# Moving the state copies of a selective scan from VectorE to ScalarE, and the written order that goes with it

## The chip, the cores and the metric

The kernel runs on one core of a Trainium2 chip. A time is the device time of one execution in microseconds. Lower is better. Of the kernel before there are three runs without the profiler and one profiled execution.

## What is computed

Four layers follow one another on an image of 4 x 64 x 64 positions with 128 channels. Layers 0 and 1 each hold a selective scan over the 4096 positions in four directions (row by row, column by column, and both backwards); layer 2 is a graph-like layer with gates over 3 x 3 neighbours, layer 3 is neighbourhood attention over 7 x 7 windows. The change concerns the scans alone. Cut to what matters:

```python
delta = jax.nn.softplus(dts)                 # per channel and position
A = -jnp.exp(A_logs)                         # per channel and state, 16 states
def step(h, inp):
    d, u, b, c = inp
    dA = jnp.exp(d[..., None] * A)
    h = dA * h + (d * u)[..., None] * b[:, :, None, :]
    y = jnp.sum(h * c[:, :, None, :], axis=-1)
    return (h, y)
```

Layer 0 scans 128 channels, layer 1 scans 256. Around the scans there are projections, a depthwise 3 x 3 convolution, normalizations and gates.

## The kernel before, in words

**Units.** A task is one batch and one block of 128 channels: 4 tasks for layer 0, 8 for layer 1. A task has 16 steps, four directions by four stretches of 1024 positions. A step has 16 units; a unit is 8 channels by 16 states, so 128 partitions, by 1024 positions. That makes 3072 units, and `Scans.run` (L477) is one loop over them, u. `manual_schedule` keeps every engine's instructions in the order in which they are written.

**A unit's work.** `load` (L388) brings the unit's delta times x from DRAM, repeated over the states (dub). `times_b` (L395) multiplies it by B on POOL into dbu, of which there are 3 buffers. `decay` (L400) spreads delta over the states by two matmuls into da, a PSUM tile of two banks with 2 buffers, and ScalarE takes the exponential in place, with A as its scale. `scan` (L410) then does three things on VectorE: the scan itself (L418), in place in da; a copy of the last column (the first, when the direction runs backwards) into states (L428), which the same unit of the next step takes as its initial value; and the product with C (L430) into hc, of which there are 6 buffers. The copy is left out in the last step of each direction, so three steps in four have it. da comes free for unit u+2 when the readers of unit u are done.

**Sums.** `add_up` (L448) sums over states on TensorE into yps, four units at a time and one half of the 1024 positions after the other. `sum_so_far` (L432) puts the y of earlier directions into yps at the start of a step, and `keep` (L463) copies yps to y on ScalarE at its end.

**Order.** In iteration u the loop writes scan(u), keep(u-2), times_b(u+3), decay(u+2), the sums, then the slot for other work, then load(u+6).

**Other work.** Into the slot go the pieces of `prepare` (L286; delta, its three bf16 parts and the repeats of B and C for a later step) and of the side work (`Side`: projections, normalizations, depthwise convolutions, what stands before and after the scans). Both are generators. Each yields the engine that its next piece needs (TAB means an activation from another table, with a table load on either side). `Plan` (L115) keeps a model clock, `at`, for PE, ACT and POOL; `slot` (L153) sets it anew in every unit from now = u x UNIT and adds the unit's own work. `Lane.fits` (L172) lets a piece in when its start plus its usual time is no later than now + UNIT + SLACK of its engine. `Counted` (L75) passes the instructions on and adds their modelled time; this is why all of other work has line L98. DMA issues of other work are put into SP's queue by `post` and `flush` when they are due by the same clock. Pieces of prepare are also forced through by their count, and side work by its pace and due times.

Of the kernel before, what the change touches and what calls it, by code (L numbers as in the profile page):

```python
# [26 lines left out]
NG = 16  # L27
TS = 1024
HALVES = TS // T
# [74 lines left out]
    return int(np.prod(t.shape[1:]))  # L104


UNIT = 3.85
USUAL = dict(PE=2.1, ACT=0.7, TAB=3.3, POOL=1.3)
SLACK = dict(PE=1.2, ACT=2.2, POOL=3.0)
LANDING = 6.0  # L110
FOUR_LANDING = 12.0
ROWS_LANDING = 12.0
# [2 lines left out]
class Plan:  # L115
# [20 lines left out]
    def post(self, chain, issue, due=0.0):  # L136

        if self.running:
            self.posted.append((chain, max(self.done, due), issue))
        else:  # L140
            issue()
# [11 lines left out]
    def slot(self, u, sums):  # L153
        at = self.at
        self.now = u * UNIT
        self.flush()
        at["PE"] = max(at["PE"], self.now) + 1.1
        at["ACT"] = max(at["ACT"], at["PE"]) + 1.1
        at["POOL"] = max(at["POOL"], self.now - 1.2) + 2.4
        at["PE"] += sums  # L160


class Lane:
# [8 lines left out]
    def fits(self, more=0.0):  # L172

        plan = self.plan
        for what in self.next.split():
# [3 lines left out]
            start = max(plan.at[kind], self.ready)  # L179
            if start + USUAL[what] > plan.now + UNIT + SLACK[kind] + more:  # L180
                return False
# [58 lines left out]
class Scans:  # L240
# [45 lines left out]
    def prepare(self, t, step):  # L286
# [40 lines left out]
        def repeat(i):  # L327
            rep = out["BC"[i]] = self.tile("rep" + "BC"[i], 2)
            src = bass.AP(xdd.tensor, xdd.offset + (R + i * NS) * TS, [[TS, NS], [0, 8], [1, TS]])
            nc.sync.dma_start(out=rep, in_=src)  # L330

        for i, free in enumerate((5, 8)):
            post("rep", lambda i=i: repeat(i), max(begin + free * UNIT, ready))

# [34 lines left out]
        def own(part, j):  # L369
            if j == part == 0:  # L370
                out["delta"] = self.tile("dp", 2, shape=(96, 4, TS), dtype=BF16)
            nc.sync.dma_start(
                out=out["delta"][32 * part : 32 * part + 32, j, :], in_=parts[32 * j : 32 * j + 32, part, :]
            )

        for i in range(12):
            j, part = divmod(i, 3)
            post("rep", lambda part=part, j=j: own(part, j), begin + (9 + 0.7 * i) * UNIT)
        yield ""
# [30 lines left out]
    def scan(self, u):  # L410
        nc = self.nc
        t, step, jj, j, g = self.unit(u)
        back = t.steps[step][0] >= 2
        way = slice(None, None, -1) if back else slice(None)
        if g == 0:
            t.states[step] = self.tile("state", 2, shape=(P, NG))
        da, dbu = self.live.pop(("da", u)), self.live.pop(("dbu", u))
        nc.vector.tensor_tensor_scan(  # L418
            da[:, way],
            da[:, way],  # L420
            dbu[:, way],
            0.0 if step % NSTEP == 0 else t.states[step - 1][:, g : g + 1],
            ALU.mult,
            ALU.add,
        )
        if step % NSTEP < NSTEP - 1:
            end = 0 if back else TS - 1
            nc.vector.tensor_copy(t.states[step][:, g : g + 1], da[:, end : end + 1])  # L428
        hc = self.live["hc", u] = self.tile("hc", 6)
        nc.vector.tensor_mul(hc, da, t.prepared[step]["C"])  # L430

# [45 lines left out]
    def run(self, between):  # L477

        total = NU * len(self.tasks)
        first = self.tasks[0]  # L480
        for _ in self.fetch(first):
            pass
        for _ in self.prepare(first, 0):
            pass
        self.plan.start()
        pieces, fetch = Lane(self.plan, iter(())), iter(())
        for u in range(-6, total):
            if u >= 0:
                self.scan(u)
            if u >= 2:  # L490
                self.keep(u - 2)
            if 0 <= u + 3 < total:
                self.times_b(u + 3)
            if 0 <= u + 2 < total:
                self.decay(u + 2)
            if u >= 0 and u % NG in (2, 3):
                self.sum_so_far(u, u % NG - 2)
            if u >= 0 and u % 4 == 3:
                self.add_up(u, 0)
            if u > 0 and u % 4 == 0:  # L500
                self.add_up(u - 1, 1)
            self.plan.slot(u, (1.6 if u % 4 in (0, 3) else 0.0) + (2.1 if u % NG in (2, 3) else 0.0))
            ahead, rest = divmod(u + AHEAD, NG)
            if rest == 0:
                while pieces.step():
                    pass
                self.plan.flush("prep", "rep")
            if rest == 0 and 0 < ahead < total // NG:
                n, step = divmod(ahead, NU // NG)
                if step == 0:  # L510
                    self.plan.flush("side")
                    fetch = self.fetch(self.tasks[n])
                    for _ in range(self.tasks[n].W.nct):
                        next(fetch, None)
                pieces = Lane(self.plan, self.prepare(self.tasks[n], step))
            next(fetch, None)
            while (pieces.count < rest - 2 or pieces.fits()) and pieces.step():
                pass
            if u >= 0:
                n, i = divmod(u, NU)  # L520
                if self.later:
                    self.later.pop(0)()
                between(n, i)
            if 0 <= u + 6 < total:
                self.load(u + 6)
        self.add_up(total - 1, 1)
        self.keep(total - 1)
        while self.later:
            self.later.pop(0)()
# [891 lines left out]
def layer2(tc, C, nb, x_in, x_out, d_w, d_rel, d_v):  # L1421
    with ExitStack() as es:
# [11 lines left out]

        with tc.manual_schedule():
            run(each(E.statistics, 0, range(8)))
            E.roots([E.rstd])
            run(each(E.project, 0, range(6)))
            E.edge_row()
            run(each(E.statistics, 1, range(2)))  # L1440
            before = last = None
            for b in range(nb):
# [392 lines left out]
```

## Time and profile before

| What | Value |
|---|---|
| median of 3 runs | 14696.81 us (14688.04 to 14710.08) |
| the profiled execution's own time | 14702.13 us |
| its span | 14700.3 us |
| mean granted TensorE clock | 0.711 |
| busy: PE, DVE, ACT, POOL | 10730.8, 12416.1, 7877.7, 9851.6 us |
| first and last start of L418 | 310.9 and 11716.3 us (the wait ahead of the first included) |
| L428, state copies | 2304, median 158 ns |
| L408, exponentials | 3072, mean 1089 ns |
| L398, times_b | 3072, mean 2354 ns |
| POOL L398 waiting for DVE L418 | 882.7 us |
| POOL L398 waiting for DMA of dub | 559.2 us |
| ACT casts to parts waiting for POOL | 278.3 us |

A row of the profile's groups gives line, engine, operation, tiles written and read, shapes and count, then busy time and mean duration, then the engine's idle time just before these instructions and what ended most of it. In a timeline, a row begins with start and duration in microseconds from the span's start, and an idle time of the engine ahead of it stands in brackets, with what ended it. Equal neighbours are merged. Waits of an engine for its own queue are not shown.

Up to 11720 us the page shows the scans, with preparation and side work between their units; after that come layers 2 and 3.

### The profile page before, as it was taken

Reading aid. Unit: us, or ns where it says so; the run is one execution under the profiler, and the core shown is the slowest. Engines: PE = TensorE matmul, PEld = TensorE weight load, DVE = VectorE, ACT = ScalarE, POOL = GpSimd, SP = SyncE. Lnnn points to the kernel's source line nnn. Section 1 sums busy time; section 2 is a strip of 40 time slices with the busy share of each in tenths; the row PEclk is TensorE's granted clock in tenths of the full one; section 3 lists DMA queues with packets and bytes.
Section 4 is the critical chain, followed back from the end, with each engine's and each line's share of the span. In section 5 each row is a group of like instructions: output and inputs, shape, how many; then the busy total and the mean of one; then the engine's idle time right before and its main releaser. Section 6 shows DMA issues by size and latency. Waiting matters only on the chain. (4 is left out here: it accounts for less than half of the span.)

```text
span 14700.3 us, 125581 instructions
## 1 busy us (share of the span) xinstructions
PE 10730.8 (73%) x36776; PEld 2755.0 (19%) x36776; DVE 12416.1 (84%) x10627; ACT 7877.7 (54%) x9279; POOL 9851.6 (67%) x4742
## 2 busy tenths in 40 slices
PE   5777777777776677777767767777776657777999
PEld 1111111111111111111111111111111112223555
DVE  1999999999999999999999999999999904565666
ACT  3645466555656565566555555555555335543555
POOL 1877788777888788788778888888888713441000
PEclk7676676766667666667667776667766568777999
DMA  4888888888888988988888777787787600002000
GB/s 113 220 207 218 204 216 222 216 214 217 216 224 215 224 208 208 230 217 211 216 213 213 199 195 200 197 208 200 196 205 193 166 30 24 20 18 48 13 14 8
DMA packets 853732, 2490.00 MB, mean 169 GB/s; under 512 B 143031, under 2 KB 164287, under 8 KB 844855
## 3 DMA queue, kind: packets, MB, share of 16 engines
q1 hardware_dynamic: 853047, 2481.97, 67.1%
q8 instruction: 295, 4.83, 0.1%
q14 instruction: 390, 3.19, 0.1%
HBM read 2060.21 MB, written 270.27 MB: 159 GB/s over the span
## 5 line engine op out<-in xcount | busy, mean ns | idle before, releaser
L398 POOL TENSOR_TENSOR dbu<-dub,repB 128x1024 f32<-128x1024 f32 x3072 | 7189.7, 2354 | 1511.2 <-DVE da L418 882.7
L418 DVE TENSOR_TENSOR_SCAN da<-da,state,dbu 128x1024 f32<-128x1024 f32 x2304 | 5415.4, 2350 | 297.3 <-ACT da L408 246.7
L408 ACT ACTIVATE da<-da,av 128x1024 f32<-128x1024 f32 x3072 | 3343.2, 1089 | 3647.8 <-PE da L406 3582.6
L406 PE MATMUL da<-dp,spread 96*128 96x512 bf16 x6144 | 2592.8, 516 | 2982.7 <-DVE hc L430 2959.1
L430 DVE TENSOR_TENSOR hc<-da,repC 128x1024 f32<-128x1024 f32 x3072 | 3741.0, 1218 | 40.5 <-PE ms L98 0.5
L453 PE MATMUL yps<-hc,gather 128*32 128x512 f32 x12288 | 2363.5, 852 | 2.3 <-DVE hc L430 2.3
L418 DVE TENSOR_TENSOR_SCAN da<-da,dbu 128x1024 f32<-128x1024 f32 x768 | 1759.2, 2291 | 400.7 <-POOL dbu L398 321.5
L406 PEld LDWEIGHTS <-spread 96*128 96x128 bf16 x6144 | 477.5, 107 | 6516.1 <-DVE hc L430 4124.8
L98 PE MATMUL ms<-d,wts 128*128 128x512 f32 (+3 forms) x960 | 782.0, 941 | 203.6 <-POOL d L98 140.7
L98 ACT ACT_TABLE_LOAD x640 | 821.1, 1283 | 126.8 <-DMA xcd<-o 90.8
L98 POOL TENSOR_TENSOR delta<-delta,low 128x1024 f32<-128x1024 f32 x192 | 452.3, 2356 | 529.9 <-ACT low L98 529.9
L98 PE MATMUL mp<-xd,dtw 8*128 8x512 f32 (+1 forms) x768 | 668.9, 965 | 28.7 <-DMA xd<-xdd 17.1
L98 ACT CAST parts<-delta 128x1024 bf16<-128x1024 f32 x384 | 400.5, 1043 | 295.8 <-POOL delta L98 278.3
L1371 POOL TENSOR_TENSOR acc<-acc,part 128x512 f32<-128x512 f32 x256 | 318.8, 1268 | 338.1 <-DVE part L1367 338.0
L446 PE MATMUL yps<-y,ident 128*128 128x512 f32 x576 | 520.3, 998 | 3.2 <-ACT y L471 3.2
L453 PEld LDWEIGHTS yps<-hc,gather 128*32 128x32 f32 x12288 | 283.9, 128 | 1190.3 <-issue 1184.5
L98 POOL TENSOR_TENSOR low<-delta,xc 128x1024 f32<-128x1024 f32 x192 | 501.1, 2610 | 1.7
L1615 ACT ACTIVATE s<-s,nmax 128x512 f32<-128x512 f32 x512 | 366.8, 718 | 248.7 <-DVE nmax L1612 243.9
L1282 ACT ACTIVATE hid<-hid,relb 128x1024 f32<-128x1024 f32 x288 | 320.3, 1145 | 323.0 <-DVE hid L1277 320.3
L98 ACT ACTIVATE low<-mp,av 128x512 f32<-128x512 f32 x384 | 264.1, 688 | 399.9 <-PE mp L98 397.7
L1277 DVE TENSOR_TENSOR hid<-cen,near 128x1024 f32<-128x1024 f32 x288 | 336.2, 1218 | 163.6 <-PE cen L1270 113.6
L98 PE MATMUL ms<-pad,diag 96*32 96x504 f32 (+1 forms) x2304 | 420.4, 824 | 64.0 <-ACT o L98 47.9
(230 smaller groups left out, 11780.3 us busy)
## 6 DMA issues: line engine op xcount, KB each, us to landing
dub<-dud SPq DMA_DIRECT2D x3072, 512.0 KB
dp<-parts SPq DMA_DIRECT2D x2304, 64.0 KB
repB<-xdd SPq DMA_DIRECT2D x192, 512.0 KB
repC<-xdd SPq DMA_DIRECT2D x192, 512.0 KB
dud<-low SPq DMA_DIRECT2D x192, 512.0 KB
pad<-xid SPq DMA_DIRECT2D x192, 256.0 KB
szd<-o SPq DMA_DIRECT2D x96, 256.0 KB
xcd<-o SPq DMA_DIRECT2D x96, 256.0 KB
```

The source lines that it names most:

```text
L98: return call(*args, **kw)
L398: self.nc.gpsimd.tensor_mul(dbu, self.live.pop(("dub", u)), t.prepared[step]["B"])
L406: self.nc.tensor.matmul(da[:, cols], self.C.spread[:, jj, :], dp[:, j, cols], start=True, stop=True)
L408: self.nc.scalar.activation(da, da, AF.Exp, scale=t.W.a[:, at : at + 1])
L418: nc.vector.tensor_tensor_scan(da[:, way], da[:, way], dbu[:, way], 0.0 if step % NSTEP == 0 else t.states[step - 1][:, g : g + 1], ALU.mu ...
L430: nc.vector.tensor_mul(hc, da, t.prepared[step]["C"])
L446: self.nc.tensor.matmul(out, lhs, self.view(rhs, k, c, i, HALVES), start=True, stop=False)
L453: self.nc.tensor.matmul(self.live["yps"][32 * j : 32 * j + 32, cols], self.C.gather[:, jj, :], self.live["hc", v][:, cols], start=False, s ...
L1277: nc.vector.tensor_add(hid.rearrange("p i (r w) -> p (i r) w", w=HW), cen[pair].rearrange("p i (r w) -> p (i r) w", w=HW), self.near[m][s] ...
L1282: nc.scalar.activation(hid, hid, AF.Gelu, bias=self.relb[:, m, t : t + 1])
L1371: nc.gpsimd.tensor_add(acc, acc, part)
L1615: nc.scalar.activation(s[:, i, :], s[:, i, :], AF.Exp, bias=nmax[:, h : h + 1], accum_out=total[:, h : h + 1],)
```

## The change

The state copy goes from VectorE to ScalarE. In the loop, decay moves from behind scan(u), as decay(u+2), to ahead of scan(u), as decay(u+1); so on ScalarE the order is the exponential of u+1, the state copy of u, keep, then the slot's work. keep, sum_so_far and add_up are written one iteration later, and the flush after the loop has both halves of the last sum. times_b and load stay where they are. In the plan UNIT goes from 3.85 to 3.7, ScalarE's slack from 2.2 to 2.4, and the model clock of ACT has a floor for the copy; POOL's line stays.

```diff
-UNIT = 3.85
+UNIT = 3.7
 USUAL = dict(PE=2.1, ACT=0.7, TAB=3.3, POOL=1.3)
-SLACK = dict(PE=1.2, ACT=2.2, POOL=3.0)
+SLACK = dict(PE=1.2, ACT=2.4, POOL=3.0)
...
         at["PE"] = max(at["PE"], self.now) + 1.1
         at["ACT"] = max(at["ACT"], at["PE"]) + 1.1
+        at["ACT"] = max(at["ACT"], self.now + 2.4) + 0.2
         at["POOL"] = max(at["POOL"], self.now - 1.2) + 2.4
         at["PE"] += sums
...
             end = 0 if back else TS - 1
-            nc.vector.tensor_copy(t.states[step][:, g : g + 1], da[:, end : end + 1])
+            nc.scalar.copy(t.states[step][:, g : g + 1], da[:, end : end + 1])
         hc = self.live["hc", u] = self.tile("hc", 6)
         nc.vector.tensor_mul(hc, da, t.prepared[step]["C"])
...
         for u in range(-6, total):
+            if 0 <= u + 1 < total:
+                self.decay(u + 1)
             if u >= 0:
                 self.scan(u)
-            if u >= 2:
-                self.keep(u - 2)
+            if u >= 3:
+                self.keep(u - 3)
             if 0 <= u + 3 < total:
                 self.times_b(u + 3)
-            if 0 <= u + 2 < total:
-                self.decay(u + 2)
-            if u >= 0 and u % NG in (2, 3):
-                self.sum_so_far(u, u % NG - 2)
-            if u >= 0 and u % 4 == 3:
-                self.add_up(u, 0)
+            if u >= 0 and u % NG in (3, 4):
+                self.sum_so_far(u, u % NG - 3)
             if u > 0 and u % 4 == 0:
-                self.add_up(u - 1, 1)
-            self.plan.slot(u, (1.6 if u % 4 in (0, 3) else 0.0) + (2.1 if u % NG in (2, 3) else 0.0))
+                self.add_up(u - 1, 0)
+            if u > 1 and u % 4 == 1:
+                self.add_up(u - 2, 1)
+            self.plan.slot(u, (1.6 if u % 4 in (0, 1) else 0.0) + (2.1 if u % NG in (3, 4) else 0.0))
...
-        self.add_up(total - 1, 1)
+        for i in range(HALVES):
+            self.add_up(total - 1, i)
         self.keep(total - 1)
```

## The prediction

> **What bounds the kernel now.** I read the page's slices and groups first, then VectorE's timeline in a stretch without stalls, then the list of waits, then two stretches of all engines. From the page:
>
> ```profile
> DVE  1999999999999999999999999999999904565666
> L418 DVE TENSOR_TENSOR_SCAN da<-da,state,dbu 128x1024 f32<-128x1024 f32 x2304 | 5415.4, 2350 | 297.3 <-ACT da L408 246.7
> L430 DVE TENSOR_TENSOR hc<-da,repC 128x1024 f32<-128x1024 f32 x3072 | 3741.0, 1218 | 40.5 <-PE ms L98 0.5
> ```
>
> VectorE is full through four fifths of the span. Those are the 3072 scan units, from 320.0 us to 11719.9 us by the first and last rows of L418 and L430: 3.711 us a unit. The rest (layers 2 and 3) is untouched. So the question is VectorE's period per unit. Its timeline, start and duration first:
>
> ```profile
> 5049.53 2.36 DVE L418 TENSOR_TENSOR_SCAN da<-da,state,dbu 128x1024 f32<-128x1024 f32 x1 [0.58 <-ACT da L408]
> 5051.92 0.16 DVE L428 COPY state<-da 128x1 f32<-128x1 f32 x1
> 5051.99 1.22 DVE L430 TENSOR_TENSOR hc<-da,repC 128x1024 f32<-128x1024 f32 x1
> 5053.13 2.35 DVE L418 TENSOR_TENSOR_SCAN da<-da,state,dbu 128x1024 f32<-128x1024 f32 x1
> 5055.51 1.22 DVE L430 TENSOR_TENSOR hc<-da,repC 128x1024 f32<-128x1024 f32 x1
> 5056.65 2.35 DVE L418 TENSOR_TENSOR_SCAN da<-da,state,dbu 128x1024 f32<-128x1024 f32 x1
> ```
>
> With the state copy a unit takes 3.60 us, without it (every fourth step) 3.52. The copy is busy 0.16 us but overlaps: the product starts 0.110 us after the scan's end with it and 0.035 without (medians over all units). It costs **0.075 us** a unit. Above this pace there are 445 us of VectorE stalls in all, mostly ScalarE's exponential arriving late; the list of waits has that, and one line from layer 3 that matters below:
>
> ```profile
> DVE da L418 <- ACT da L408: 321.6, 314, 8.3
> ACT inv L1641 <- PE ps L1639: 26.6, 52, 3.3
> ```
>
> **What the Trainium skill says.** "PSUM — Partial Sum Buffer", section "PSUM bank collisions raise a hardware error": two engines may not touch one bank and 32-partition quadrant at once, two reads included, and accesses are to be guarded by bank, not address. The trace shows that the program is ordered this way: L1641 reads ps[:, 0, :], yet what releases it is L1639, which writes ps[:, 1, :], other columns of the same bank. No row shows two readers. "ScalarE: Activation LUTs", section "What ACT_TABLE_LOAD costs", gives 186 ns plus 0.833 ns per element for an ACTIVATE with immediates and 1283 ns for a table load; here PSUM copies of 512 and 128 elements take 587 and 267 ns (the same slope, 160 ns at zero elements), and the load takes 1283. The PSUM page's "Engine vs sequencer instructions" calls ScalarE's queue strictly first in, first out; the rows below agree.
>
> **The change, part by part.**
>
> *The copy leaves VectorE.* Gain 2304 x 0.075 = 173 us if nothing takes its place. But da lies in two PSUM banks and the product L430 reads both. The copy on ScalarE, written ahead of it, reads a column of one. So I expect **the product to wait for the copy**: the 0.110 us between scan and product becomes hand-off to ScalarE, copy, hand-off back. VectorE to ScalarE takes 0.035 us (L1277 to L1282) or 0.095 (L1612 to L1615), the copy 0.161 (from the line above), ScalarE to VectorE 0.033 (L1641 to L1643) or 0.103 (L408 to L418). Sum 0.229 to 0.359, net of 0.110: +0.12 to +0.25 us; I take 0.17. **2304 x 0.17 = 390 us** (274 to 574).
>
> *The copy sits behind the next unit's exponential.* Until now an exponential had until its own scan starts. Now exp(u+1) must be over when scan(u) ends, 1.2 us earlier, or it holds the copy, and the copy holds product u. A place where this costs nothing today:
>
> ```profile
> 5098.79 1.28 ACT L98 ACT_TABLE_LOAD   x1
> 5100.02 2.35 DVE L418 TENSOR_TENSOR_SCAN da<-da,state,dbu 128x1024 f32<-128x1024 f32 x1
> 5100.08 0.69 ACT L98 ACTIVATE o<-ms,v 128x512 f32<-128x512 f32 x1
> 5100.79 1.28 ACT L98 ACT_TABLE_LOAD   x1
> 5102.08 1.09 ACT L408 ACTIVATE da<-da,av 128x1024 f32<-128x1024 f32 x1
> 5102.40 1.23 DVE L430 TENSOR_TENSOR hc<-da,repC 128x1024 f32<-128x1024 f32 x1
> ```
>
> A Silu between two table loads (3.26 us) delays the exponential to 5103.17, 0.8 us after the scan's end at 5102.37; VectorE doesn't notice, as the next scan starts at 5103.54. In a copying unit the product would have been held 0.8 us. Taking end of exp(u+1) minus end of scan(u) from these rows for every unit: it is over zero in 45% of all, and in 1062 of the 2304 copying ones; in a quiet unit it is -0.48. The positive part sums to 1026 us over copying units; 311 of this is stall of the next scan that is paid today already, leaving 715. A hold lets ScalarE and TensorE catch up, so lateness that carries from one unit to the next counts once: 489. Two corrections oppose each other: the unit is 0.17 us longer, which takes some 100 us off; and side work now begins after the copy, 0.7 us later than after the exponential. Side work that fits a unit without a hold shrinks from 4.2 us to 2.45 (from the copy's end, 2.5 us after the last product, to 4.9): 67 stretches between exponentials hold more than 4.2 today, 368 in copying steps hold more than 2.4, by 333 us in sum. The planner's new lines do not forbid that: ACT work may end at now + 6.1 (3.7 + 2.4) where the held product asks for 4.9 (now is the last product's end; scan(u+1) ends 6.0 us later, and exp(u+2) ahead of its copy takes 1.09). I take **550 us** (350 to 900).
>
> *Decay moved to the head of the loop.* The da matmul and exponential keep their order among themselves, as sums, written one unit later, keep theirs against the da matmuls. What moves is **side work and preparation**: on PE and ACT they now stand one exponential earlier, while POOL's stand behind the same times_b, which waits for the same scan; the plan's POOL line (now - 1.2) is not moved. So a POOL result used by ACT or PE arrives a unit later in their terms:
>
> ```profile
> 5113.80 2.36 POOL L398 TENSOR_TENSOR dbu<-dub,repB 128x1024 f32<-128x1024 f32 x1 [1.56 <-DVE da L418]
> 5116.13 2.34 POOL L98 TENSOR_TENSOR delta<-delta,low 128x1024 f32<-128x1024 f32 x1
> 5118.51 1.05 ACT L98 CAST parts<-delta 128x1024 bf16<-128x1024 f32 x1 [1.73 <-POOL delta L98]
> 5119.46 1.08 ACT L408 ACTIVATE da<-da,av 128x1024 f32<-128x1024 f32 x1
> 5121.96 2.29 DVE L418 TENSOR_TENSOR_SCAN da<-da,dbu 128x1024 f32<-128x1024 f32 x1
> ```
>
> Standing one exponential earlier, this cast would hold the exponential of the scan at 5118.43 until about 5119.6: 2.3 us late. Over the 587 such hand-offs (380 casts, 72 ACT and 135 PE users of side tiles) the same reckoning gives 747 us if POOL keeps its times; 433 if POOL's backlog (times_b starts 2.7 us after its scan in the median) shrinks as VectorE is held; 156 if POOL also gains what it waits for ACT today. Many fall into holds already counted: **200 us** (50 to 450).
>
> *Other edits, together.* keep moves from ahead of an exponential to behind the copy (stalls in that slot are 109 us now, units 3 of 16): no more than it gives back, as 1.47 us of y copy still stands in the shorter window. SP's stores and dub loads keep their order against POOL; 67 us of scan waits for dbu should fade with longer units: -50 us. The smaller UNIT packs side work no more loosely: nothing. The matmul of da(u+2) also waits for the copy now, which is over before product u: nothing.
>
> Sum: 14702.1 (span 14700.3 plus 1.8 around it) + 390 + 550 + 200 - 50 = 15792, less 5 for the median of the runs: **15,790 us**.
>
> **Rivals.**
> 1. *Hand-off only.* The planner's new ACT floor keeps exponentials early enough: 14697 + 390, and up to half of the 550: 15,090 to 15,350. For it: in 55% of units the exponential is early. Against: 300-odd table-load pairs of 3.26 us exceed 2.45.
> 2. *The product does not wait* (faster). Two reads are left unordered; the copy is hidden: 14697 - 173, and 60 off for the keep slots: about 14,460; with some POOL lateness, 14,600. It decides if the product starts about 0.035 us after the scan. For it: no row shows two readers ordered. Against: the skill's rule and L1641.
> 3. *No wait, but POOL lateness rules:* 14697 - 173 + 200 to 430 = 14,720 to 14,950.
> 4. *Everything adds:* no catching up, 574 + 900 + 450: 16,600.
>
> **How the numbers follow.** Forecast 0.65 (own range 15,350 to 16,400), rival 1 0.17, rival 2 0.05, rival 3 0.05, rival 4 0.08. The range 15,150 to 16,450 leaves out rivals 2 and 3, most of 4 and an edge of 1. A difference of 0.2% (30 us) is about what can be told from none. Faster is rival 2, 0.05; the same 0.02, an edge of 3; slower 0.93.
>
> **What would show it.** Right: L430 shows idle time released by an ACT row of the copy line, some 900 us or more; the product starts 0.25 us or more after the scan in copying steps and 0.035 in others; units in copying steps are longer than 3.59 us even without stalls of the scan; ACT casts and PE side matmuls wait longer for POOL. Wrong: L430 without such waits (rivals 2 and 3), or waits of 0.2 us with no long tail (rival 1).

## The result, and the profile after

The change is slower: 15,767.88 us in the median of 4 runs (15,763.88 to 15,777.51), 14,697.60 us before; the ratio is 1.0729, interval 1.071 to 1.0747. The prediction was 15,790 us. The profiled execution took 15,764.78 us, of which its span is 15,762.5.

All of the 1,070 us lie in the scans: from the first scan's start to the last product's end it is 12,460 us instead of 11,400, so 4.056 us a unit instead of 3.711. From the page:

```profile
DVE  1888888888888888888888888888888842555666
L419 DVE TENSOR_TENSOR_SCAN da<-da,state,dbu 128x1024 f32<-128x1024 f32 x2304 | 5414.1, 2350 | 152.5 <-ACT da L409 143.2
L431 DVE TENSOR_TENSOR hc<-da,repC 128x1024 f32<-128x1024 f32 x3072 | 3763.2, 1225 | 1592.3 <-ACT state L429 1551.7
L429 ACT COPY state<-da 128x1 f32<-128x1 f32 x2304 | 373.8, 162 | 325.3 <-DVE da L419 262.2
```

VectorE is no longer full: nines have become eights. The idle time ahead of the scan (L419) is halved, and a new one of 1,592 us stands ahead of the product (L431), where there were 40 us; nearly all of it ends with ScalarE's state copy. The list of VectorE's waits gives time, number and longest:

```profile
DVE hc L431 <- ACT state L429: 1551.7, 2304, 17.4
...
DVE da L419 <- ACT da L409: 155.7, 125, 7.1
```

The wait comes 2,304 times, once for every copy. Two neighbouring units in the timeline (rows of VectorE and ScalarE alone), the first held by a late exponential, the second not:

```profile
5053.90 2.29 DVE L419 TENSOR_TENSOR_SCAN da<-da,dbu 128x1024 f32<-128x1024 f32 x1
5054.70 0.69 ACT L98 ACTIVATE sq<-ms,bias 128x512 f32<-128x512 f32 x1
5055.55 1.09 ACT L409 ACTIVATE da<-da,av 128x1024 f32<-128x1024 f32 x1 [0.17 <-PE da L407]
5056.57 0.16 ACT L429 COPY state<-da 128x1 f32<-128x1 f32 x1
5056.76 1.23 DVE L431 TENSOR_TENSOR hc<-da,repC 128x1024 f32<-128x1024 f32 x1 [0.57 <-ACT state L429]
5057.10 1.04 ACT L98 CAST parts<-delta 128x1024 bf16<-128x1024 f32 x1 [0.37 <-POOL delta L98]
5057.90 2.29 DVE L419 TENSOR_TENSOR_SCAN da<-da,dbu 128x1024 f32<-128x1024 f32 x1
5058.69 1.09 ACT L409 ACTIVATE da<-da,av 128x1024 f32<-128x1024 f32 x1 [0.54 <-PE da L407]
5060.23 0.16 ACT L429 COPY state<-da 128x1 f32<-128x1 f32 x1 [0.45 <-DVE da L419]
5060.42 1.23 DVE L431 TENSOR_TENSOR hc<-da,repC 128x1024 f32<-128x1024 f32 x1 [0.23 <-ACT state L429]
```

In the second unit ScalarE waits for the scan (0.45 us), copies, and the product starts 0.225 us after the scan's end. In the first the exponential ends at 5056.64, 0.45 us after the scan's end at 5056.19; copy and product move with it, to 0.57. Over all 2,304 copying units the start of the product behind the scan adds up to 1,552 us, where it was 253: 0.225 us in the quiet units (the median is 0.226), over 0.35 us in 790 of them. The 768 units without a copy start their product after 0.035 us in the median, as before. Against these +1,299 us stand stalls ahead of scans that have gone (450 to 191 us; a stall is what a scan starts later behind the last product than in the quiet case), and the product itself is 7 ns longer than before (1,218 to 1,225 ns, 22 us in all): 1,299 - 259 + 22 = 1,062 us, which is the growth of the scan part (1,060) within 2 us.

### The profile page after: what moved, and what is told of

The parts are those of the page before. It is cut to its first block, busy times and chain, and to the rows that moved or that the text cites. A ratio compares the mean times of both kernels' runs of the same rounds, so it can differ in the third digit from the quotient of the medians.

```text
span 15762.5 us, 126031 instructions
## 1 busy us (share of the span) xinstructions
PE 11081.7 (70%) x36776; PEld 2795.0 (18%) x36776; DVE 12231.0 (78%) x8323; ACT 8165.0 (52%) x11583; POOL 9889.1 (63%) x4742
## 5 line engine op out<-in xcount | busy, mean ns | idle before, releaser
L419 DVE TENSOR_TENSOR_SCAN da<-da,state,dbu 128x1024 f32<-128x1024 f32 x2304 | 5414.1, 2350 | 152.5 <-ACT da L409 143.2
L407 PE MATMUL da<-dp,spread 96*128 96x512 bf16 x6144 | 2692.3, 534 | 3547.5 <-DVE hc L431 3505.0
L431 DVE TENSOR_TENSOR hc<-da,repC 128x1024 f32<-128x1024 f32 x3072 | 3763.2, 1225 | 1592.3 <-ACT state L429 1551.7
L454 PE MATMUL yps<-hc,gather 128*32 128x512 f32 x12288 | 2491.9, 896 | 2.3 <-DVE hc L431 2.3
L419 DVE TENSOR_TENSOR_SCAN da<-da,dbu 128x1024 f32<-128x1024 f32 x768 | 1757.2, 2288 | 318.9 <-POOL dbu L399 306.3
L98 PE MATMUL ms<-d,wts 128*128 128x512 f32 (+3 forms) x960 | 817.7, 980 | 179.9 <-POOL d L98 115.4
L98 ACT CAST parts<-delta 128x1024 bf16<-128x1024 f32 x384 | 402.5, 1048 | 560.0 <-POOL delta L98 526.1
L429 ACT COPY state<-da 128x1 f32<-128x1 f32 x2304 | 373.8, 162 | 325.3 <-DVE da L419 262.2
L98 PE MATMUL ms<-pad,diag 96*32 96x504 f32 (+1 forms) x2304 | 457.7, 891 | 52.8 <-ACT o L98 37.0
```

The costliest lines, as they stand in the source:

```text
L98: return call(*args, **kw)
L407: self.nc.tensor.matmul(da[:, cols], self.C.spread[:, jj, :], dp[:, j, cols], start=True, stop=True)
L419: nc.vector.tensor_tensor_scan(da[:, way], da[:, way], dbu[:, way], 0.0 if step % NSTEP == 0 else t.states[step - 1][:, g : g + 1], ALU.mu ...
L429: nc.scalar.copy(t.states[step][:, g : g + 1], da[:, end : end + 1])
L454: self.nc.tensor.matmul(self.live["yps"][32 * j : 32 * j + 32, cols], self.C.gather[:, jj, :], self.live["hc", v][:, cols], start=False, s ...
```

## The experiments

Each time below is the median of 4 runs (13 in number 8). The ratio is to runs of the kernel before that were made beside them, with its 95% interval.

The theory: the product waits for ScalarE's copy (hand-off), the copy for the next exponential (lateness; the time by which it delays the product is a hold), and side work on PE and ScalarE now stands a unit ahead of POOL's. The main rival: what costs is the moved order with its constants, the copy is a side issue.

**1. Order and plan alone.** The change with its copy back on VectorE:

```diff
-            nc.scalar.copy(t.states[step][:, g : g + 1], da[:, end : end + 1])
+            nc.vector.tensor_copy(t.states[step][:, g : g + 1], da[:, end : end + 1])
```

> The changed kernel with its state copy back on VectorE: written order and plan of the change alone. Theory (the product waits for ScalarE's copy, and the copy for a late exponential): no holds of the product, so most of the 1071 us go; what stays is side work that waits a unit longer for POOL, 14,700 to 15,000 us. Rival (the moved order and the plan cost the time, the copy is a side issue): 15,400 us or more.

Measured: 15,146 us, ratio 1.0301 (1.0286 to 1.0317). Between the two theories: 440 us are order and plan, 622 us the copy. The holds of the product are gone, but stalls ahead of scans have doubled from 450 to 895 us. In the lists of waits the scan's wait for the exponential was 321.6 us before, and ScalarE's casts (the bf16 parts of delta) waited 278.3 us for POOL:

```profile
DVE da L419 <- ACT da L409: 797.5, 500, 17.4
...
ACT parts L98 <- POOL delta L98: 644.5, 260, 8.1
```

**2. The copy alone,** in the kernel before, with its order: the same two lines exchanged the other way round.

> The kernel before with its state copy on ScalarE, order and plan untouched: the copy of unit u then stands behind the side work of the slot too. Theory: the product is held by that side work as well; a mean of 1.05 us of it stands between exponentials and only some 0.4 us is free, so about 0.7 us more a copying unit: 16,300 to 16,900 us, slower than the change. Rival (the order costs the time): 14,700 plus the hand-off of 265, about 14,960 us.

Measured: 17,505 us, ratio 1.1903 (1.1885 to 1.192). Here the copy stands behind the slot's side work, and the product is held by that too:

```profile
DVE hc L430 <- ACT state L428: 3377.2, 2304, 7.2
```

This is more than I expected: 3,124 us above the 253 of the kernel before, instead of some 1,900. Two things were larger than I had taken them. In the median the next exponential ends only 0.05 us before the scan, so the 0.4 us of free time isn't there. And side work also waits, 1,059 us for PE and only 49 for POOL, and those waits hold the copy like its own busy time does. The rival fails. A copy that stands behind the next exponential alone costs far less (15,336 us, number 12), so that part of the new order is no cause of the loss; what the order costs by the place of side work is a matter of its own (1, 9, 10).

**3. The product ahead of the copy,** in the change: the two lines of the product are written ahead of the copy.

> The changed kernel with the product written ahead of ScalarE's copy: the copy now waits for the product, not the product for the copy. Theory: the product starts 0.035 us after the scan in every unit, the holds of 1299 us vanish, but the copy keeps ScalarE waiting to the product's end and frees da some 0.25 us later, so stalls ahead of scans return in part: 14,600 to 15,100 us. Rival (ScalarE is simply overloaded by the 2304 copies and their waits, wherever they stand): 15,500 us or more.

Measured: 15,314 us, ratio 1.0412 (1.0395 to 1.043), above the range of the theory, which had left the 440 us of the first experiment out, and below the rival's. Against that one it is 168 us slower. The product does start 0.035 us after the scan in the median (every fourth unit 0.104); the wait turns round, and stalls ahead of scans grow from 895 to 1,169 us:

```profile
ACT state L431 <- DVE hc L428: 1959.0, 1632, 9.9
DVE da L419 <- ACT state L431: 803.2, 525, 17.1
```

ScalarE waits for the product's end in 1,632 units, so its side work and with it the next exponential come late. The second row names the copy, but it is the exponential that these scans waited for: the copy of u stands right behind the exponential of u+1, and in the median of the 525 waits the scan starts 0.102 us after the exponential's end, its usual hand-off, and 0.015 us after the copy's, less than any hand-off here (0.032 and more). So in either order one engine waits for the other, but not at the same price: against the first experiment the copy costs 168 us behind the product and 622 ahead of it.

**4 and 5. The plan's POOL line moved on by a unit,** in the change and in the first experiment:

```diff
-SLACK = dict(PE=1.2, ACT=2.4, POOL=3.0)
+SLACK = dict(PE=1.2, ACT=2.4, POOL=6.7)
...
-        at["POOL"] = max(at["POOL"], self.now - 1.2) + 2.4
+        at["POOL"] = max(at["POOL"], self.now + 2.5) + 2.4
```

> The changed kernel with the plan's POOL line moved on by a unit (now + 2.5 instead of now - 1.2) and POOL's slack by 3.7. Theory: side pieces behind a POOL result are let in a unit later, so the part of the holds in which ScalarE waited for POOL (200 us in the trace, and part of the PE ones) shrinks: 15,500 to 15,680 us. Rival (POOL's place plays no part): within 30 us of 15,768.

> The first experiment (state copy back on VectorE, order and plan of the change, 15,146 us) with the plan's POOL line moved on by a unit as well. Theory: of the 440 us that order and plan cost, the part in which ScalarE waited for POOL (some 225 us more than before in its trace) goes: 14,850 to 14,980 us. Rival (DMA landings and the plan's tighter constants cost the 440): above 15,080 us.

Measured: 15,652 us (1.0643, 1.0627 to 1.0659) in the change, 116 us less, and 15,123 us (1.0285, 1.0271 to 1.0299) in the first experiment, 23 us less. The theory holds for the first and fails for the second, where the rival's range holds. The waits of casts for POOL did fall (644.5 to 305.7 us, and 526.1 to 200.4 in the change), but in the second kernel ScalarE's waits for the stores of o and sq to land, xcd, szd and xid, rose from 159.2 to 344.5 us. More of the gain went where side work falls due, at unit 233 of a task: stalls in units 228 to 242 rose from 145 to 235 us, TensorE's side matmuls in units 230 to 240 from 272 to 457 us, and the longest wait of a scan is 50.3 us:

```profile
DVE da L419 <- ACT da L409: 735.8, 389, 50.3
```

In the change the stalls and holds of the same units rose from 151 to 232 us. So the later line seems to leave more pieces to be forced in at the end. Whether the stores are late for want of SP's order or for this reason is not shown. Another cure was tried below (10).

**6. The product in halves,** the PSUM bank that the copy doesn't read first:

```diff
-        nc.vector.tensor_mul(hc, da, t.prepared[step]["C"])
+        for i in range(HALVES) if not back else reversed(range(HALVES)):
+            cols = self.half(i)
+            nc.vector.tensor_mul(hc[:, cols], da[:, cols], t.prepared[step]["C"][:, cols])
```

> The changed kernel with the product cut in two halves of 512 positions, the bank without the copied column first. Theory (the order is by PSUM bank): the first half starts 0.035 us after the scan, and the copy and its hand-offs hide behind its 0.7 us; two halves cost about 0.05 us more than one product: 15,150 to 15,500 us. Rival (the order is by tile, both halves wait): 15,850 us or more.

Measured: 15,896 us, ratio 1.0814 (1.0799 to 1.0828). The rival holds. VectorE's timeline, with both halves merged:

```profile
4998.33 2.35 DVE L419 TENSOR_TENSOR_SCAN da<-da,state,dbu 128x1024 f32<-128x1024 f32 x1
5000.90 1.29 DVE L433 TENSOR_TENSOR hc<-da,repC 128x512 f32<-128x512 f32 x2 [0.22 <-ACT state L429]
```

The first half already waits for the copy, 0.225 us as the whole product did, and the second follows it at once. So the program's order is kept for the whole tile, not bank by bank.

**7. No state copies,** in the kernel before; the recurrence is cut between stretches, and each scan starts from the constant zero. The copy's lines go, and:

```diff
-            0.0 if step % NSTEP == 0 else t.states[step - 1][:, g : g + 1],
+            0.0,
```

> The kernel before without the state copies: each stretch of 1024 positions starts from zero, so the recurrence is cut between stretches; all else is done. It measures what a copy costs on VectorE. Theory: 0.075 us each, 14,698 - 173 = 14,525 us if the stalls stay; 14,560 if part of it turns into stalls. Rival (a copy costs its whole 0.158 us): 14,330 us.

Measured: 14,598 us, ratio 0.9928 (0.9913 to 0.9944): 105 us less, above both figures of the theory and far above the rival's. It is not the clean measure that I wanted, since a scan that starts from a constant is shorter too, 2,287 instead of 2,349 ns. The shortest period with nothing late falls to 3.463 us, from 3.525 without a copy and 3.590 with one in the kernel before. These two differ by 0.065 us and not by 0.075: the copy delays the product's start by 0.075, but the product behind a copy is 10 ns shorter (1,215 against 1,225 ns). Of the roughly 255 us of VectorE's work that this takes away, 148 come back as stalls ahead of scans (450 to 598 us). So even a copy that cost nothing would probably have gained well under 2304 x 0.065 = 150 us: the engines that feed VectorE are close behind.

**8. Only keep behind decay,** in the kernel before, with 1.5 us for it in the plan:

```diff
-            if u >= 2:
-                self.keep(u - 2)
             if 0 <= u + 3 < total:
                 self.times_b(u + 3)
             if 0 <= u + 2 < total:
                 self.decay(u + 2)
+            if u >= 2:
+                self.keep(u - 2)
...
+            self.plan.copy = u >= 2 and (u - 2) % NG == NG - 1
...
+        at["ACT"] += 1.5 * self.copy
```

> The kernel before with one thing taken from the change: the copy of y is written behind the exponential of the same iteration instead of ahead of it, and the plan counts 1.5 us on ScalarE for it in that slot. The state copy stays on VectorE. Theory: most of the 109 us of stalls in the unit behind it go: 14,590 to 14,670 us. Rival (the copy of y delays the next exponential just as much): 14,680 to 14,720 us.

Measured: 14,705 us, ratio 1.0 (0.9992 to 1.0008): no difference. The theory fails; the rival's range holds, but not its reason. The stalls in the unit behind the copy of y do fall, from 110 to 42 us, but the sum of all stalls stays (450 and 449 us); other units of a step take them over. The prediction had rightly given this edit nothing.

**9 and 10. Order and constants apart.** Number 9 is the first experiment with UNIT, ScalarE's slack and its clock line of before. Number 10 is the first experiment with the constants of the change, but with times_b and load written a unit later too:

```diff
-            if 0 <= u + 3 < total:
-                self.times_b(u + 3)
+            if 0 <= u + 2 < total:
+                self.times_b(u + 2)
...
-            if 0 <= u + 6 < total:
-                self.load(u + 6)
+            if 0 <= u + 5 < total:
+                self.load(u + 5)
```

> The first experiment (copy on VectorE, written order of the change, 15,146 us) with UNIT, ScalarE's slack and ScalarE's clock line as before. It parts order from constants. Theory (side work on PE and ACT standing a unit ahead of POOL's and of SP's is what costs): 15,000 to 15,200 us, most of the 440 stays. Rival (the tighter constants cost it): 14,680 to 14,850 us.

> The first experiment with times_b and load also written a unit later (times_b(u+2), load(u+5)), so that POOL's and SP's side work stand to the scans as PE's and ScalarE's do; plan constants of the change, copy on VectorE. Theory: it is the order of before under other numbers, so the 440 us go but for what the constants cost: 14,680 to 14,850 us. Rival (the constants cost it): 15,000 us or more.

Measured: 14,852 us (1.0104, 1.0089 to 1.0119) and 14,861 us (1.0112, 1.0095 to 1.0129). Number 10 lies just above what its theory gave, number 9 just above what its rival gave: neither order nor constants alone is the cause. Order costs 152 us by itself, the constants 161, and together they cost 440, so some 130 us come only from both. That the 161 are the constants' rests on number 10 having the order of before in all that counts; the same order with the old constants was not run. What the constants do shows in part at the end of tasks. The timeline of number 10 near the due time of side work, at unit 235 of a task (TensorE's matmuls, the exponential and the scan):

```profile
3163.63 8.27 PE L98 MATMUL ms<-pad,wts 128*64 128x512 f32 x24 [0.79 <-ACT o L98]
...
3172.84 1.97 PE L98 MATMUL ms<-d,wts 64*64 64x512 f32 x4 [0.94 <-ACT d L98]
3174.74 1.04 PE L407 MATMUL da<-dp,spread 96*128 96x512 bf16 x2
3175.81 1.09 ACT L409 ACTIVATE da<-da,av 128x1024 f32<-128x1024 f32 x1 [0.22 <-PE da L407]
3177.00 2.36 DVE L419 TENSOR_TENSOR_SCAN da<-da,state,dbu 128x1024 f32<-128x1024 f32 x1 [15.81 <-ACT da L409]
```

A stretch of convolution pieces (24 matmuls in 8.3 us, then four more) stands ahead of one pair of da matmuls, and the scan waits for 15.8 us. In units 228 to 242 of the tasks stalls sum to 34 us before and 116 here, 82 of the 161, and TensorE's side matmuls in units 230 to 240 to 213 and 270 us. My reading is that with less room in a unit fewer pieces fit, and what is left over is forced in when it is due. Where the other half arises was not traced. Counting all stalls above 4 us, 78 and 215, would give 137 of the 161, but number 8 has 139 us of them in the time of the kernel before, so that count can't place a cost. The three constants (UNIT, ScalarE's slack and its clock line) were not taken apart.

**11 and 12. The change aligned.** Number 11 is the change with the edit of number 10; number 12 has the old constants besides, so that of the whole change only the copy on ScalarE, behind the next exponential and ahead of the slot's work, and the place of keep are left.

> The change itself, copy on ScalarE, with times_b and load written a unit later as in the experiment beside it. What is left is the copy's own price: hand-off 265 us and the holds by late exponentials without those by late POOL results and DMA landings. Theory: 15,300 to 15,550 us. Rival (the two costs are one and the same lateness, so that aligning gives nothing while the product is held): 15,650 us or more.

> The experiment before (change with times_b and load written a unit later) with UNIT, ScalarE's slack and ScalarE's clock line of before as well: what is left of the change is the state copy on ScalarE behind the next exponential and ahead of the slot's work. If the prices add, it is 14,700 plus the 596 us between the two aligned runs (15,457 - 14,861), of which 265 hand-off: 15,250 to 15,350 us, and the constants' 160 us go. Rival (under the held product the constants no longer matter, since longer units give side work its time): 15,400 to 15,460 us.

Measured: 15,457 us (1.0513, 1.0498 to 1.0529) and 15,336 us (1.0432, 1.0415 to 1.045). Both agree with the theory. The product's wait for the copy falls with each step, 1,552 us in the change, then:

```profile
DVE hc L431 <- ACT state L429: 1317.9, 2304, 17.5
```

and in number 12:

```profile
DVE hc L430 <- ACT state L428: 1215.8, 2304, 10.7
```

So the 1,070 us fall into three parts: from 14,698 to 15,336 the copy itself (about 640), to 15,457 the constants (121), to 15,768 the place of POOL's and SP's work against PE's and ScalarE's (311). The parts depend somewhat on the order in which they are undone. The copy costs 640 with order and constants out of the way, 596 between 10 and 11, 622 between 1 and the change; the place of the work costs 285 between 10 and 1. In units 228 to 242 stalls and holds are 67 us in number 12 and 119 in number 11, so here too some half of what the constants cost lies at the due time. The casts' wait for POOL goes 526.1 to 126.8 us with the last of these undone.

## Why the prediction was right, step by step

- **The product waits for the copy:** right, and shown: 2,304 waits, and both turning the order round (3) and taking the copy back (1) remove them. My reason was half right. I argued from PSUM banks; the runs show an order by tile (6). The two columns of L1641 and L1639 lie in one tile too, so that line could not tell the two apart. The rule that I cited from the Trainium skill ("PSUM — Partial Sum Buffer", section "PSUM bank collisions raise a hardware error") asks for a guard by bank; this program waits more widely than that, as the halves of number 6 show with their 0.225 us.
- **Hand-off, 390 us:** too large. It is 0.225 - 0.110 = 0.115 us, so 265 us. The measured legs are 0.034 and 0.032 us with a copy of 0.160; of the two values that the trace offered for each leg the short one held both times, and I had taken the middle. The longer product adds 22 us, which I count with the lateness. My 0.075 us for the copy on VectorE was a little too much as well (0.065, see 7).
- **Lateness, 550 us:** the mechanism right, the size too large where it can be read alone. In number 12 it is 640 - 265, about 375 us after the stalls that it replaces (the product's 22 us in it). In the change's trace the holds beyond 0.225 us sum to 1,033 us: sorted by what the late exponential had ahead of it, 334 us have a late da matmul, 257 ScalarE's own load (194 of it table-load pairs), 200 a wait for POOL, 199 a wait of side work for PE, 42 for a DMA. My list had the table loads foremost; late da matmuls are larger.
- **Side work a unit ahead of POOL, 200 us:** right in its cause, too small: 311 us in the change, 152 alone with the old constants. ScalarE's casts wait longer for POOL, as I had said; but the other sign, PE side matmuls that wait longer for POOL, failed: in the scans they wait 75 us in the change and 96 before. I had counted hand-offs from POOL only. SP's transfers shift by a unit as well, which I had set at nothing; side matmuls wait 239 us for landings in the change, 98 before, and when POOL's waits were planned away (5), ScalarE's waits for landings grew. How much of the 311 is SP's is open.
- **The smaller UNIT, nothing:** wrong, as far as it can be told from the other two constants, which went back with it. Together they cost 121 us in the change and 161 without the copy, about half of it at the due time of side work, where pieces that fell behind are forced in. I had asked only whether pieces could be packed more tightly, not what happens to those that no longer fit.
- **Gains, -50 us:** scan waits for dbu went from 366.8 to 313.5 us, as said; keep's place gave nothing (8).

That 15,790 us came so near to 15,768 is luck: errors of both signs met, 125 and 175 us too much on the copy, 111 and 121 too little on order and constants, and the 50 of the gains, which the 375 already contain. The path itself, product behind copy behind exponential, was right. Rivals 2 and 3 (no wait) are refuted by the 2,304 waits, rival 4 (everything adds, 16,600 us) by the time. Rival 1 (hand-off and half of the lateness, 15,090 to 15,350 us) gives the time of number 12, the copy with almost nothing else, not that of the change. No version here beats the kernel before, apart from the one that leaves the copies out.

What stays open: the 130 us that order and constants cost only together were not taken apart, nor were the places of POOL's and of SP's work; number 10 moves both. The product written ahead of the copy (3) was tried only with the order and constants of the change, not in the aligned order, where the copy on ScalarE might cost least. And the part of the granted TensorE clock is open: in the scans it is 0.68 before, 0.65 in the change and 0.61 in number 2, and a da matmul takes 516 ns before and 534 in the change:

```profile
L406 PE MATMUL da<-dp,spread 96*128 96x512 bf16 x6144 | 2592.8, 516 | 2982.7 <-DVE hc L430 2959.1
L407 PE MATMUL da<-dp,spread 96*128 96x512 bf16 x6144 | 2692.3, 534 | 3547.5 <-DVE hc L431 3505.0
```

In the slower kernels here the clock is mostly lower. Whether it adds to the late da matmuls or only goes with the longer time is not shown.

## What to carry to other kernels

Here a small operation that went to another engine cost not its own time but two hand-offs and everything that stood ahead of it in that queue, because the bottleneck read the same tile next. Before such a move, ask who else reads the tile, which of the two readers is written first (behind the product the same copy cost 168 us instead of 622), and when the new engine is free. When a step moves in a written order, list which engines' queues move with it: a queue left behind shows up as waits between two engines that are both off the critical path. Moving the planner's line alone gave 116 and 23 us here, moving the written order 311 and 285. And a tighter pacing constant is not safer, since what no longer fits may be forced in later, in one piece.

## What the runs showed of the hardware that I had not expected

- In this program the product waits for a copy of one column even where it reads only the other half of a tile of two banks: 0.225 us in the quiet unit, as for the whole (6). That is an order of the program; the runs don't show what the memory itself would allow.
- The state copy on VectorE is busy for 158 ns but adds 65 ns to a quiet unit: it delays the product's start by 75 ns, and the product behind it takes 1,215 ns, 1,225 where it follows the scan without a copy on VectorE (the change and 7).
- A scan that starts from a constant takes 2,287 ns, one that starts from a column in SBUF 2,349.
